# First stage of a fused attention kernel: weights fetched in column parts, x on two DMA queues, rows normalised on VectorE, and one bias transpose moved to a later stage

## The chip, the cores and the metric

The kernel runs on one core of a Trainium2 chip. A core has five engines that each take their own instructions in order: TensorE (PE, with weight loads shown apart as PEld), VectorE (DVE), ScalarE (ACT), GpSimd (POOL) and SyncE (SP), and 16 DMA engines that move data between device memory and the on-chip memory. A DMA is issued by an engine's instruction stream; here nearly all are issued by SP. The metric is the device time of one execution in microseconds (us); the times shown are medians of several executions.

## The reference

The reference is a stack of four small transformer blocks in float32, applied to x of shape (8, 112, 256) with a context of shape (8, 375, 192):

```
L0:  x += Attn(LN(x), LN(x));  x += Attn(LN(x), ctx);  x += (a * gelu(gate)) @ Wf      16 heads of 64
L1:  the same with other weights and tanh-gelu                                        16 heads of 64
L2:  x += Attn(LN(x), ctx)                                                            16 heads of 64
L3:  x += SelfAttn(LN(x)), masked, biased;  x += Attn(LN(x), ctx), masked, biased;
     x += gelu(LN(x) @ W1 + b1) @ W2                                                  16 heads of 16
```

Attn(h, c) is softmax(q k^T * scale) v with q = h Wq, k = c Wk, v = c Wv over 16 heads, then a product with Wo and a bias. Only block L3 has biases on its q and k projections. That makes ten stages, numbered 0 to 9: self, cross, ff, self, cross, ff, cross, self, cross, ff. Stage 0 is the self-attention of L0 and stage 6 is the attention of L2.

## The kernel before

**Tiles.** The 896 rows of x lie in seven tiles of 128 rows (`x_sb[t]`, loaded at L319 by seven DMAs of 128 KB). For each stage `norm(st, t)` (L495) computes mean and variance of a tile on VectorE (`st`, `mv`, `ve`, lines 498 to 502), the inverse root `rs` on GpSimd (L504), the normalised rows `xn` on GpSimd (L506), and then adds the output bias row of the stage into the tile (L507, GpSimd). The function behind `add_norm_transposes` transposes `xn` on TensorE (L520) and evicts it with the norm's gain and bias into `hT` (L299 on ScalarE or L307 on VectorE). Tiles go in groups 0 and 1, 2 and 3, 4 and 5, 6. Projections to q and k (L581) work on column blocks of two batches (j = 0 to 3); values (L605) on one batch and half of the heads; scores (`S`, L818), softmax (L783 maximum, L793 exponential, L803 reciprocal, L804 normalisation on GpSimd), transposes of the probabilities (`T`, L837) and the product with the values (`PV`, L857) work on eight heads of one batch in stages 0 and 3. The work of 16 such steps fills stage 0.

**Order.** TensorE's instructions stand in the order in which the program emits them (`manual_schedule`). The order is made while the program is built, by the class `Plan`: every piece of work is an `Item` with a cost, a deadline (in steps), the tiles that it uses and makes, and dependences with delays. The main loop emits S, T and PV of the steps and fills between them with the ready item of the earliest deadline. `plan.now` is the planner's own clock and `plan.ev` the time on it at which a piece was done; nothing of this exists on the chip. The instructions of the other engines are put in order by the framework's scheduler; on each engine they then run in that order, and one that waits holds those behind it. That scheduler goes by its own estimates: a load without dependences can stand far ahead of the place where the program emits it. The two `rv` rows, which come after the masks of the last block in the list of loads, are issued at 42.56 and 43.03 us, long before the masks.

**Loads.** Weights live in a ring of seven buffers. Loads are `Item`s in a first-in-first-out list; `pump` issues the first one as soon as its ring has room. All of them are issued by SP: Wq1, Wk1 and Wv1 of block L0 (L370, each [256, 1024] as one DMA of 1 MB with rows of 4 KB), the context in three parts (`cn`, L412, 125 partitions with pieces of 768 bytes), Wo1 (L370, rows of 1 KB) between the first two of them, then bias rows (L402) and two value-bias rows (`rv`, L1121 and L1123). The framework uses eight completion semaphores for these DMAs in turn, so that a DMA is issued when the one eight before it has landed.

**Biases of the last block.** `brows` holds the q and k biases of L3, 16 rows of 64 values. It is cleared on GpSimd (L343), loaded by a DMA that GpSimd issues (L344), scaled on GpSimd (L345, L346), transposed on TensorE (L349) and copied to `bcols` (L350). In the program this stands ahead of everything else on TensorE but the transpose of the norm vectors (`vrows`, L331). `bcols` is first used in stage 7.

Of the kernel before, what the change touches and what calls it, by code (L numbers as in the profile page):

```python
# [12 lines left out]
ALU = mybir.AluOpType  # L13
AX = mybir.AxisListType

B, T, D = 8, 112, 256
S, DC = 375, 192
# [3 lines left out]
P = 128  # L21
# [241 lines left out]
def kernel(ctx: ExitStack, tc: tile.TileContext, a: dict, out: bass.AP):  # L263
    nc = tc.nc
# [17 lines left out]
    def mm_tile():  # L282
        return ps_m.tile([P, 512], F32, tag="mm", name="mm")

    plan = Plan(RINGS)
    load = {"act": 0.0, "dve": 0.0}

    def busy(eng, us):
# [25 lines left out]
    xflat = a["x"].rearrange("b t d -> (b t) d")  # L314
    oflat = out.rearrange("b t d -> (b t) d")
    x_sb = []
    for t in range(NT):
        xt = const.tile([P, D], F32, name=f"x{t}")
        nc.sync.dma_start(xt, xflat[t * P : (t + 1) * P, :])  # L319
        x_sb.append(xt)  # L320

    ident = const.tile([P, P], F32, name="ident")
# [17 lines left out]


    brows = const.tile([16, 4, 32], F32, name="brows")
    nc.gpsimd.memset(brows, 0.0)  # L343
    nc.gpsimd.dma_start(brows[:, :, 0:16], a["padb"].rearrange("r (h d) -> r h d", d=16))  # L344
    nc.gpsimd.tensor_scalar_mul(brows[0:8, :, :], brows[0:8, :, :], 0.25)  # L345
    nc.gpsimd.memset(brows[0:8, :, 16:17], 1.0)  # L346
    bcols = const.tile([P, 16], F32, name="bcols")
    pt1 = mm_tile()
    nc.tensor.transpose(pt1[:, :16], brows.rearrange("r h d -> r (h d)"), ident[:16, :16])  # L349
    nc.vector.tensor_copy(bcols, pt1[:, :16])  # L350

    hT = const.tile([P, 2, B * T], F32, name="hT")

# [9 lines left out]
    got = {}  # L363


    def add_w(key, name, cols=None, kp=P):
        def fn():
            w = a[name] if cols is None else a[name][:, cols]
            t = wpool.tile([kp, w.shape[0] // kp, w.shape[1]], F32, tag="w", name=name)
            nc.sync.dma_start(t, w.rearrange("(c p) n -> p c n", p=kp))  # L370
            got[key] = t

        plan.add_load(Item(("load", key), 0, fn, makes=[key]))
# [24 lines left out]
    def add_row(key, name):  # L398
        def fn():
            t = rpool.tile([P, D], F32, tag="row", name="row")  # L400
            r = ROWS.index(name)
            nc.sync.dma_start(t, a["rows"][r : r + 1, :].to_broadcast([P, D]))  # L402
            got[key] = t

        plan.add_load(Item(("load", key), 0, fn, makes=[key]))
# [56 lines left out]
    def add_masks():  # L462
# [16 lines left out]
        def put_mask():  # L479
# [7 lines left out]
                 deps=[(("kj", 6, B - 1, u), 0) for u in range(4)] + [(("vj", 6, B - 1, i), 0) for i in range(3)],  # L487
                 seg=SEG[7])
        )
# [5 lines left out]
    def norm(st, t):  # L495
        xt = x_sb[t]
        s6 = small.tile([P, 6], F32, tag="st", name="st")
        nc.vector.bn_stats(s6, xt)
        mv = small.tile([P, 2], F32, tag="mv", name="mv")
        nc.vector.bn_aggr(mv, s6)  # L500
        ve = small.tile([P, 1], F32, tag="ve", name="ve")
        nc.vector.tensor_scalar_add(ve, mv[:, 1:2], EPS)  # L502
        rs = small.tile([P, 1], F32, tag="rs", name="rs")
        nc.gpsimd.tensor_tensor(rs, ve, mhalf, ALU.pow)  # L504
        xn = xpool.tile([P, D], F32, tag="xn", name="xn")
        nc.gpsimd.tensor_scalar(xn, xt, mv[:, 0:1], rs, ALU.subtract, ALU.mult)  # L506
        nc.gpsimd.tensor_add(xt, xt, got[("row", st)])  # L507
        busy("dve", 0.8)
        xns[(st, t)] = xn

    def add_norm_transposes(st, g, bt, deadline, first=False):
        for gi, ts in enumerate(GROUPS):

            def fn(gi=gi, ts=ts):
# [8 lines left out]
                for c in range(2):  # L523
# [7 lines left out]
                    ("hT", st, gi), 0.22 * len(ts), fn, deadline(gi),  # L531
                    deps=[(("norm", st, t), 4.5) for t in ts], seg=SEG[st],
                )
# [205 lines left out]
    def add_context_transposes(deadline):  # L739
        for b in range(B):  # L740
            key = ("w", "ctx", b // 3)

            def fn(b=b, key=key):
                cn = got[key]
                cols = slice(b * S, (b + 1) * S)
                for k0, kl, dst in ((0, KA, ctxA), (KA, KB, ctxB)):
                    pc = mm_tile()
                    for c in range(3):
                        nc.tensor.transpose(
                            pc[:kl, c * CH : (c + 1) * CH],  # L750
                            cn[:, (b % 3) * 3 + c, k0 : k0 + kl], ident[:CH, :CH],
                        )
                    evac(dst[:kl, cols], pc[:kl, :S], S)
                nc.sync.dma_start(ctxB[KB:, cols], ctxB[:KB, cols])

            plan.add(Item(("ctxT", b), 0.7, fn, deadline(b), uses=[key]))

# [204 lines left out]


    info = []
    SEG = [0, 0, 0, 1, 1, 1, 2, 2, 2, 2]
    for kind, dh in (
        ("self", 64), ("cross", 64), ("ff", 0), ("self", 64), ("cross", 64), ("ff", 0),
        ("cross", 64), ("self", 16), ("cross", 16), ("ff", 0),  # L970
# [1 line left out]
        st = len(info)  # L972
# [19 lines left out]
    def self_stage(st, names, wq, wk, wv, wo):  # L992
        kind, first, per, dh = info[st]
        L3 = dh == 16
        us = 2 if L3 else 4
# [65 lines left out]
    def w(name):  # L1061
        return ("w", name)
# [9 lines left out]
    st = 0  # L1072
    for bi, (L, n) in enumerate(seq):
        s0, s1, s2 = st, st + 1, st + 2
        add_row(("row", s0), n[4])
        for i in range(3):
            add_w(w(n[i]), n[i])
        if bi == 0:
            add_ctx(0, [0, 1, 2])
        add_w(w(n[3]), n[3])  # L1080
        if bi == 0:
            add_ctx(1, [3, 4, 5])
            add_ctx(2, [6, 7])
        add_w(w(n[7]), n[7])
        add_ctx_w(w(n[8]), n[8], True)
        add_ctx_w(w(n[9]), n[9], False)
        add_row(("row", s1), n[11])
        add_w(w(n[10]), n[10])
        add_w(("w", n[14], "g"), n[14], slice(FF, 2 * FF))
        add_w(("w", n[14], "a"), n[14], slice(0, FF))  # L1090
        add_row(("row", s2), n[16])
        add_w(w(n[15]), n[15])

        f0, f1, f2 = info[s0][1], info[s1][1], info[s2][1]
        add_norm_transposes(s0, n[5], n[6], hT_by(s0))
        self_stage(s0, n, w(n[0]), w(n[1]), w(n[2]), w(n[3]))
        add_products(s0, s1, w(n[3]), 8, after_pv(f0, 2), norm_by(s1))
        add_norm_transposes(s1, n[12], n[13], hT_by(s1))
        if bi == 0:
            add_context_transposes(lambda b: f1 + 4 * b - 5 if b > 1 else 7 + b)  # L1100
        cross_stage(s1, w(n[7]), w(n[8]), w(n[9]), 0.125, None)
        add_products(s1, s2, w(n[10]), 8, after_pv(f1, 4), norm_by(s2))
        add_norm_transposes(s2, n[17], n[18], hT_by(s2))
        ff_stage(s2, ("w", n[14], "a"), ("w", n[14], "g"), n[19],
                 AF.Gelu if bi == 0 else AF.Gelu_apprx_tanh, f2 - 1)
        add_products(s2, s2 + 1, w(n[15]), 8, after_ff(s2), ff_norm_by(f2))
        st += 3
# [6 lines left out]
    add_ctx_w(w(L + "Wv"), L + "Wv", False)  # L1114
    add_w(w(L + "Wo"), L + "Wo")
    add_masks()
    L3 = "L3_xattn_"

    def add_rvs():
# [38 lines left out]
    for t in range(NT):  # L1158
        norm(0, t)
        plan.refs[("row", 0)] = plan.refs.get(("row", 0), 0)  # L1160
        plan.ev[("norm", 0, t)] = 1.0

    cuts = [0, info[2][1], info[5][1], len(steps)]
    for seg in range(3):
# [11 lines left out]
        for i in range(lo - 2, hi):  # L1176
# [6 lines left out]
            if lo <= i + 1 < hi:  # L1183
                n = steps[i + 1]
# [44 lines left out]
```

## Time and profile before

| What | us |
|---|---|
| median of three runs | 1757.38 (1756.21 to 1757.70) |
| profiled execution | 1756.8 |
| its span | 1755.0 |
| TensorE busy in the span | 1696.6 (97%) |
| start of the first projection matmul (L581) | 23.55 |
| start of the first GpSimd normalisation (L804) | 46.75 |
| start of the first probability transpose (L837) | 52.75 |

A line of the profile gives the source line, the engine, the operation, what it writes and reads, the count, the busy time and the mean duration of one; behind the bar stands the idle time of the engine just before it and what ended that. In a timeline the columns are start, duration, engine and line, and in brackets the idle time before with what released it. "SPq" is the instruction stream of SP, where a DMA's duration is the time that its issue held SP. The span leaves out 1.8 us that the profiled execution's own time holds.

### The profile page before, as it was taken

Reading aid. Unit: us, or ns where it says so; the run is one execution under the profiler, and the core shown is the slowest. Engines: PE = TensorE matmul, PEld = TensorE weight load, DVE = VectorE, ACT = ScalarE, POOL = GpSimd, SP = SyncE. Lnnn points to the kernel's source line nnn. Section 1 sums busy time; section 2 is a strip of 40 time slices with the busy share of each in tenths; the row PEclk is TensorE's granted clock in tenths of the full one; section 3 lists DMA queues with packets and bytes.
Section 4 is the critical chain, followed back from the end, with each engine's and each line's share of the span. In section 5 each row is a group of like instructions: output and inputs, shape, how many; then the busy total and the mean of one; then the engine's idle time right before and its main releaser. Section 6 shows DMA issues by size and latency. Waiting matters only on the chain.

```text
span 1755.0 us, 30348 instructions
## 1 busy us (share of the span) xinstructions
PE 1696.6 (97%) x11886; PEld 1186.7 (68%) x11886; DVE 874.6 (50%) x2046; ACT 756.1 (43%) x2410; POOL 906.6 (52%) x825
## 2 busy tenths in 40 slices
PE   5999999999999999999999999999999998999989
PEld 4877766666658887666666656666666876666656
DVE  1454454555522444554555522445555588666740
ACT  2553443444521544434444431444444366555641
POOL 4223455566702322655466612645566845888880
PEclk9999999999999999999999999999999999999999
DMA  5011011000101101000000101100000101000000
GB/s 176 11 48 53 3 29 54 25 1 1 49 27 43 28 10 40 25 28 1 25 1 1 43 28 9 10 1 1 7 1 7 12 9 55 1 1 2 1 1 22
DMA packets 39464, 39.12 MB, mean 22 GB/s; under 512 B 16928, under 2 KB 34568, under 8 KB 39321
## 3 DMA queue, kind: packets, MB, share of 16 engines
q1 hardware_dynamic: 39257, 37.13, 7.6%
q8 instruction: 94, 1.54, 0.4%
q14 instruction: 49, 0.40, 0.1%
q0 software_dynamic: 64, 0.05, 0.0%
HBM read 35.48 MB, written 0.92 MB: 21 GB/s over the span
## 4 chain that ended last, share of the span: by engine, by line
PE 85%; POOL 6%; ACT 4%; DVE 4%; issue 1%; DMA 0%; SPq 0%; ACTq 0%; POOLq 0%; DVEq 0%
PE mm L581 11%; PE mm L549 11%; PE mm L837 9%; PE s L818 9%; PE mm L857 9%; PE mm L677 7%; PE mm L643 7%; PE mm L1030 7%; PE mm L686 4%; PE mm L652 4%; POOL pr L800 4%; PE mm L605 3%; ACT pr L793 3%; DVE nm L783 2%; POOL xn L506 1%; PE mm L728 1%
## 5 line engine op out<-in xcount | busy, mean ns | idle before, releaser
L800 POOL TENSOR_SCALAR pr<-pr,rinv 112x375 f32<-112x375 f32 x512 | 623.5, 1236 | 366.2 <-DVE rinv L799 362.8
L793 ACT ACTIVATE pr<-s,nm 112x375 f32<-112x375 f32 (+1 forms) x768 | 373.5, 501 | 240.4 <-DVE nm L783 166.6
L783 DVE TENSOR_REDUCE nm<-s 112x2 f32<-112x750 f32 (+1 forms) x288 | 266.2, 953 | 68.3 <-PE s L818 63.9
L837 PE MATMUL mm<-ident,pr 112*128 112x112 f32 (+2 forms) x1920 | 241.3, 265 | 13.1 <-POOL pr L800 5.2
L837 PEld LDWEIGHTS mm<-ident,pr 112*128 112x128 f32 (+2 forms) x1920 | 214.5, 152 | 58.3 <-issue 15.5
L303 ACT COPY wT<-mm 128x448 f32<-128x448 f32 (+2 forms) x285 | 150.1, 534 | 190.5 <-PE mm L837 190.2
L857 PEld LDWEIGHTS mm<-wT,v 128*64 128x64 f32 (+5 forms) x3840 | 160.3, 129 | 84.6 <-issue 32.5
L804 POOL TENSOR_TENSOR pr<-pr,rinv 112x896 f32<-112x896 f32 x48 | 80.8, 1683 | 253.7 <-DVE rinv L803 228.1
L818 PE MATMUL s<-kT,qT 64*112 64x375 f32 (+3 forms) x1792 | 207.6, 392 | 0.0
L857 PE MATMUL mm<-wT,v 128*64 128x112 f32 (+5 forms) x3840 | 200.1, 264 | 7.4 <-ACT wT L303 4.5
L818 PEld LDWEIGHTS s<-kT,qT 64*112 64x112 f32 (+1 forms) x1792 | 113.1, 172 | 68.2 <-issue 15.3
L793 ACT ACTIVATION_READ_ACCUMULATOR pr<-s,nm 112x1 f32 x768 | 158.0, 206 | 0.0
L799 DVE RECIPROCAL rinv<-sums 112x1 f32<-112x1 f32 x512 | 83.4, 163 | 98.7 <-ACT pr L793 88.1
L311 DVE COPY kT<-mm 128x375 f32<-128x375 f32 (+1 forms) x117 | 65.5, 560 | 133.4 <-PE mm L652 114.4
L311 DVE COPY wT<-mm 128x448 f32<-128x448 f32 (+2 forms) x195 | 118.6, 612 | 21.3 <-PE mm L837 18.2
L311 DVE COPY v<-mm 128x512 f32<-128x512 f32 (+2 forms) x75 | 51.8, 691 | 141.2 <-PE mm L686 118.7
L303 ACT COPY kT<-mm 128x375 f32<-128x375 f32 (+1 forms) x107 | 51.1, 478 | 129.0 <-PE mm L652 115.3
L504 POOL TENSOR_TENSOR rs<-ve,mhalf 128x1 f32<-128x1 f32 x70 | 39.4, 564 | 126.1 <-DVE ve L502 123.9
L553 DVE TENSOR_TENSOR x<-mm,x 128x256 f32<-128x256 f32 x70 | 29.5, 422 | 143.2 <-PE mm L549 143.1
L643 PE MATMUL mm<-ctxA,L_xattn_Wk 128*128 128x375 f32 x256 | 91.5, 480 | 0.0
L677 PE MATMUL mm<-L_xattn_Wv,ctxA 128*128 128x512 f32 (+1 forms) x192 | 90.7, 595 | 0.4 <-ACT hT L299 0.4
L506 POOL TENSOR_SCALAR xn<-x,mv,rs 128x256 f32<-128x256 f32 x70 | 85.8, 1226 | 7.7 <-PE mm L520 1.1
(130 smaller groups left out, 2349.4 us busy)
## 6 DMA issues: line engine op xcount, KB each, us to landing
L_xattn_Wq<-in_L_xattn_Wq_dram SPq DMA_DIRECT2D x3, 1024.0 KB, 6.7
L_xattn_Wo<-in_L_xattn_Wo_dram SPq DMA_DIRECT2D x3, 1024.0 KB, 15.9
L_xattn_w_ff<-in_L_xattn_w_ff_dram SPq DMA_DIRECT2D x3, 1024.0 KB, 5.6
L_xattn_Wp<-in_L_xattn_Wp_dram SPq DMA_DIRECT2D x2, 1024.0 KB, 7.5
L_xattn_wq<-in_L_xattn_wq_dram SPq DMA_DIRECT2D x2, 1024.0 KB, 5.0
L_xattn_wo<-in_L_xattn_wo_dram SPq DMA_DIRECT2D x2, 1024.0 KB, 5.7
L_xattn_mlp_w<-in_L_xattn_mlp_w_dram SPq DMA_DIRECT2D x2, 1024.0 KB, 4.9
cn<-in_ctx_dram SPq DMA_DIRECT2D x2, 843.8 KB
```

The costliest lines, as they stand in the source:

```text
L303: nc.scalar.copy(dst, src)
L311: nc.vector.tensor_copy(dst, src)
L549: nc.tensor.matmul(ps[:, :D], lhsT=oT[:, c, t * P : (t + 1) * P], rhs=got[w][:, c, :], start=(c == 0), stop=(c == n - 1),)
L581: nc.tensor.matmul(ps[:, i * 2 * T : (i + 1) * 2 * T], lhsT=got[w][:, k, m * P : (m + 1) * P], rhs=hT[:, k, lo:hi], start=(k == 0), stop=( ...
L643: nc.tensor.matmul(ps[:, :S], lhsT=got[w][:, (2 * u + i) * P : (2 * u + i + 1) * P], rhs=ctxA[:, cols], start=True, stop=False,)
L677: nc.tensor.matmul(ps[: KCH[c][1], :], lhsT=lhs(ctxA, slice(0, KA), c), rhs=got[w][:, hf * 512 : (hf + 1) * 512], start=True, stop=False,)
L783: nc.vector.tensor_reduce(nm[:, :, :ns], sv, AX.X, ALU.max, negate=True)
L793: nc.scalar.activation(pr[:, bk, sl, :], sv[:, bk, sl, :], AF.Exp, bias=nm[:, bk, sl : sl + 1], accum_out=sums[:, bk, sl : sl + 1],)
L800: nc.gpsimd.tensor_scalar_mul(pr[:, bk, sl, :], pr[:, bk, sl, :], rinv[:, bk, sl : sl + 1])
L818: nc.tensor.matmul(tiles[i][:, n % 2, (n // 2) * nk : (n // 2 + 1) * nk], lhsT=qap(h), rhs=kap(h), start=True, stop=True,)
L837: nc.tensor.transpose(pt[:kl, i * T : (i + 1) * T], cell[h][:, c * P : c * P + kl], ident[:T, :T])
L857: nc.tensor.matmul(po[p0 : p0 + dp, blk * T : (blk + 1) * T], lhsT=got[vk][:kl, hv * dp : (hv + 1) * dp], rhs=wt, start=(c == 0), stop=(c ...
```

## The change

Five things are done, all in the first stage but the last one:

1. The first two tiles of x are loaded through SP, the other five and the bias row of stage 0 through ScalarE's DMA queue.
2. Wq1 and Wk1 of block L0 are loaded as four DMAs of 256 columns each, Wv1 as two of 512 columns.
3. In stage 0 `xn` is computed on VectorE instead of GpSimd.
4. The planner is told that the norms of stage 0 end one after another (1.0 + 2.0 t on its clock) and that its clock stands at 9.0 when the steps begin; the context transposes of batch b may not be emitted before step 1 + b // 3.
5. The load and the scaling of `brows` become a load item in the list of loads, behind the masks and ahead of the value-bias rows, with the DMA issued by SP. The transpose into `bcols` becomes an item of stage 6.

```diff
-        nc.sync.dma_start(xt, xflat[t * P : (t + 1) * P, :])
+        (nc.sync if t < 2 else nc.scalar).dma_start(xt, xflat[t * P : (t + 1) * P, :])
...
     brows = const.tile([16, 4, 32], F32, name="brows")
-    nc.gpsimd.memset(brows, 0.0)
-    nc.gpsimd.dma_start(brows[:, :, 0:16], a["padb"].rearrange("r (h d) -> r h d", d=16))
-    nc.gpsimd.tensor_scalar_mul(brows[0:8, :, :], brows[0:8, :, :], 0.25)
-    nc.gpsimd.memset(brows[0:8, :, 16:17], 1.0)
     bcols = const.tile([P, 16], F32, name="bcols")
-    pt1 = mm_tile()
-    nc.tensor.transpose(pt1[:, :16], brows.rearrange("r h d -> r (h d)"), ident[:16, :16])
-    nc.vector.tensor_copy(bcols, pt1[:, :16])
+
+    def load_brows():
+        nc.gpsimd.memset(brows, 0.0)
+        nc.sync.dma_start(brows[:, :, 0:16], a["padb"].rearrange("r (h d) -> r h d", d=16))
+        nc.gpsimd.tensor_scalar_mul(brows[0:8, :, :], brows[0:8, :, :], 0.25)
+        nc.gpsimd.memset(brows[0:8, :, 16:17], 1.0)
+
+    def put_bcols():
+        pt1 = mm_tile()
+        nc.tensor.transpose(pt1[:, :16], brows.rearrange("r h d -> r (h d)"), ident[:16, :16])
+        nc.vector.tensor_copy(bcols, pt1[:, :16])
...
-    def add_w(key, name, cols=None, kp=P):
+    def add_w(key, name, cols=None, kp=P, parts=1):
         def fn():
             w = a[name] if cols is None else a[name][:, cols]
+            n = w.shape[1] // parts
             t = wpool.tile([kp, w.shape[0] // kp, w.shape[1]], F32, tag="w", name=name)
-            nc.sync.dma_start(t, w.rearrange("(c p) n -> p c n", p=kp))
+            for i in range(parts):
+                c = slice(i * n, (i + 1) * n)
+                nc.sync.dma_start(t[:, :, c], w[:, c].rearrange("(c p) n -> p c n", p=kp))
             got[key] = t
...
-            nc.sync.dma_start(t, a["rows"][r : r + 1, :].to_broadcast([P, D]))
+            (nc.scalar if key[1] == 0 else nc.sync).dma_start(t, a["rows"][r : r + 1, :].to_broadcast([P, D]))
...
-        nc.gpsimd.tensor_scalar(xn, xt, mv[:, 0:1], rs, ALU.subtract, ALU.mult)
+        (nc.vector if st == 0 else nc.gpsimd).tensor_scalar(xn, xt, mv[:, 0:1], rs, ALU.subtract, ALU.mult)
...
-            plan.add(Item(("ctxT", b), 0.7, fn, deadline(b), uses=[key]))
+            plan.add(Item(("ctxT", b), 0.7, fn, deadline(b), uses=[key], deps=[(("S", 1 + b // 3), 0)]))
...
-            add_w(w(n[i]), n[i])
+            add_w(w(n[i]), n[i], parts=1 if bi else (4, 4, 2)[i])
...
     add_masks()
+    plan.add_load(Item(("load", "brows"), 0, load_brows))
+    plan.add(Item(("bcols", 0), 0.1, put_bcols, info[6][1] + 8, deps=[(("load", "brows"), 10.0)], seg=SEG[6]))
...
-        plan.ev[("norm", 0, t)] = 1.0
+        plan.ev[("norm", 0, t)] = 1.0 + 2.0 * t
+    plan.now = 9.0
```

## The prediction

> **What bounds the kernel now.** I read the page's busy times first: TensorE works 97% of the span, so time is won only where TensorE stands still, and that is at the start. The stretches of the first 60 us show it (us, then busy time of PE, PEld, DVE, ACT, POOL with counts, granted clock, DMA share, GB/s):
>
> ```profile
> PE 1696.6 (97%) x11886; PEld 1186.7 (68%) x11886; DVE 874.6 (50%) x2046; ACT 756.1 (43%) x2410; POOL 906.6 (52%) x825
> 0.00:16.00 16.00, 0.36 (x1) 0.18 (x1) 4.62 (x22) 1.28 (x1) 12.23 (x25) 1.00 0.75 263
> 16.00:23.55 7.55, 4.09 (x14) 2.45 (x15) 1.41 (x4) 1.69 (x3) 6.52 (x7) 1.00 0.36 103
> 23.55:27.87 4.32, 4.32 (x13) 3.92 (x13) 0.81 (x2) 1.00 (x2) 1.05 (x2) 1.00 0.89 245
> 27.87:52.75 24.88, 24.88 (x142) 22.03 (x141) 4.88 (x7) 10.14 (x37) 1.68 (x1) 1.00 0.30 84
> ```
>
> Until 23.55 TensorE does 4.45 us of transposes; from there it never pauses. The chain that ended last, in its first 24 us, says why: the bias row's DMA (4.01 to 10.28), then GpSimd's row additions, `rs`, `brows` and `xn` up to 23.24, each `xn` 1.21 us. The weights are not what is late: Wq1, issued at 4.49, lands 8.5 us later, at 13.0. So up to 12 us can be won here, 0.7%.
>
> The second thing to read is SP, because the change moves a DMA onto it, and the groups of the bias row and GpSimd:
>
> ```profile
> 5.99 1.01 SPq L412 DMA_DIRECT2D cn<-in_ctx_dram  x1
> 7.04 15.86 SPq L370 DMA_DIRECT2D L_xattn_Wo<-in_L_xattn_Wo_dram  x1
> 22.95 13.54 SPq L412 DMA_DIRECT2D cn<-in_ctx_dram  x2
> 36.54 5.98 SPq L402 DMA_DIRECT2D row<-in_rows_dram  x2
> ...
> L402 SPq DMA_DIRECT2D row<-in_rows_dram x1: 5507/5507/5507, 36.5 to 36.5; - x1
> DMA to landing us min/median/max: 11.1/11.1/11.1
> ...
> 46.75 1.68 POOL L804 TENSOR_TENSOR pr<-pr,rinv 112x896 f32<-112x896 f32 x1 [22.14 <-DVE rinv L803]
> 52.75 0.55 PE L837 MATMUL mm<-ident,pr 112*112 112x112 f32 x4
> ```
>
> SP is held for 35 us: each DMA behind a context part is taken only when that part is nearly through, and the bias row issued at 36.54 lands at 36.54 + 11.1 = 47.6. Between 28 and 37 us, with a context part alone in flight, the DMA share is 0.34 at 100 GB/s. The last two lines give the slack of the first softmax: normalised at 48.43, read by TensorE (T of step 0) at 52.75, so 4.3 us to spare.
>
> **What the Trainium skill says.** "DMA: Bandwidth & Descriptors", section "Why a DMA increments its semaphore by 16 and not by 1": a DMA uses the largest number of engines up to 16 that divides the slowest dimension of both sides. 125 context partitions give 5 engines, and 5/16 = 0.31 agrees with the 0.34; the 16 rows of `brows` give all 16, the five busy ones among them. The same page, "Issuing engines are not separate DMA queues": the second queue saves issue time, not bandwidth; no run here shows it yet. "TensorE: Matmul & The Clock Gate", Part 1: after some 3.4 us of idleness the array runs at half clock until a window of that length has been busy. The trace agrees: the first 11 projection matmuls last 581 ns (23.55 to 27.87), those after 352.
>
> **The change part by part.**
>
> *Start of TensorE.* Only the transposes of tiles 0 and 1 now stand before the first projections. On VectorE, `xn` of 128x256 comes after all seven statistics (7 x 0.43 + `mv`, `ve`: some 4.3 us from 2.9, so 7.2). No row prices `xn` there: below by 0.2 us, half the 0.42 of the two-tensor addition of that shape (L553); above by the 1.21 of GpSimd. I take 0.4. But in VectorE's order the first eviction of its half of `hT` stands behind `xn` of tiles 3 and 4, and that of tile 4 waits for an `rs` that GpSimd makes after four row additions of 0.71: 7.6 + 0.7 x 4 + 0.55 + 0.4 + 0.55 = 12 us, or 14.5 if the row lands as late as 10.3 again. Projections then start at 12 to 14.5 instead of 23.55.
>
> *Weights in parts.* Rows of 1 KB go at 253 GB/s at a DMA share of 0.92 (24 to 28 us, Wo1), so 275 at full share; rows of 4 KB at 384 (8 to 14 us). x, row, Wq1, Wk1 are 3.15 MB: 10.9 us at 290; Wv1, 1.05 MB in rows of 2 KB, at 340 (between the two): 3.1. From 2.0 this ends at 16.0, about when the weights end now (share 0.41 in 16 to 18). The parts are on time: TensorE needs the last of Wk1 at 24, Wv1 at 26. What follows is shifted by 0 to +2 us; I take +0.5.
>
> *`brows`: the part that decides.* GpSimd's order in the built program is: four `rs`, `brows` clear, additions to tiles 0 to 3, three `rs`, addition to tile 4, **scaling of `brows`**, clear, additions to tiles 5 and 6, then the softmax normalisations. The scaling waits for the DMA of `brows`, and that stands on SP behind all three context parts, Wo1 and the next bias row. So it lands just after that row: 47.6 + 0.1 + 0.5 = 48.2. Everything behind it on GpSimd waits: 0.75 (scaling 0.55, clear 0.10, gaps), two additions 1.40, normalisation of step 0 1.69, together 3.9 and 0.1 to TensorE: T of step 0 starts at L + 4.0 = 52.2 with L the landing. Before it was 52.75. TensorE comes to it at about 12 + 2.1 (half clock) + its work of 27 = 41 to 44 and stands still for 8 to 11 us: the whole gain of the start is spent there.
>
> *What is left at that point.* Up to T of step 0 the old order does 14 projection groups, 2 value tiles and all 14 transposes; the new one 12, 3 and 8. Still to do: 2 x 1.51 - 1.72 + 6 x 0.19 = +2.4 us. And TensorE has gone cold: from 23.55 to 27.87 half clock cost 4.3/2 = 2.15; I take the same again, between 1.7 and 3.4 by the page's windows, 0 if idleness doesn't cool it.
>
> *The rest at nothing.* The removed transpose of `brows` at the head (0.28) lay in TensorE's idle time; in stage 6 it is 0.3 us of TensorE at most. The planner's new order ends with stage 0; all later work stands in the same order but for `bcols` and its neighbours in stage 6. Six DMA issues on ScalarE, 0.43 each, end by 5, before its first work at 7.1. Context transposes come at 75 us and later, their data by 48. Behind the wait on GpSimd, the exponentials of step 1 go on, its normalisation follows that of step 0 by 1.69, and its T comes some 8 us later, so there is no second stall.
>
> *Sum.* (52.2 - 52.75) + 2.4 + 2.15 = +4.0 us on the profiled execution: span 1759.0, its time 1760.8. It lies 0.6 under the median of the runs, so the median becomes 1757.4 + 4.0 = 1761.4.
>
> **The rivals.** *A shorter stall.* If `brows` lands two us after SP takes it (42.1 + 2.4 = 44.5), as it would if its pieces met no queue, T starts at 48.5: -4.25 + 2.4 + 2.15 = +0.3, and with no cooling -1.9: 1755.5 to 1757.7. Against it: all four rows issued between 36 and 43 us land 5.8 to 11.1 us after issue.
>
> *GpSimd isn't held.* The change does what it seems to do: T of step 0 starts when TensorE reaches it, 41.5 to 44: -11.2 + 2.4 = -8.9, or -6.4: 1748.5 to 1751. This needs L below 37.5 to 40, so that GpSimd is through by then; the balance with cooling is L - 44.2, so faster by 0.2% needs L below 40.7. For it: the start really frees 9 to 12 us. Against it: SP isn't free before 42, unless the context parts go through faster than now.
>
> *A longer stall.* Weight parts at 240 GB/s instead of 290 put 2.5 us on L: 1764.
>
> **How the numbers follow.** Long stall as worked out: 0.6, own range 1758.5 to 1764.5 (shift -0.5 to +2, cooling 0.7 to 3.4). Shorter stall: 0.23. GpSimd not held: 0.13. Longer stall: 0.04. A measurement of this kernel can tell about 0.2%, 3.5 us, from no change. Slower by more, above 1760.9: two thirds of the first case and all of the last, 0.45. Faster: the third case, 0.13. Between: 0.42. The range 1754 to 1766 leaves out the third case and little else.
>
> **What would show it.** Right: GpSimd's line for the scaling of `brows` with a wait of 25 us or more on the DMA; projections from 12 to 14.5; one pause of TensorE of 8 to 11 us ahead of the first L837 transposes near 52, matmuls of 581 ns after it. Wrong: first normalisation on GpSimd before 42, no pause, or `cn` parts through by 35. Also wrong: 1 KB parts that arrive so slowly that the projections wait for Wk1.

## The result and the profile after

The changed kernel takes 1756.24 us, the median of 14 runs (1753.20 to 1759.81), beside 1756.20 (1754.35 to 1757.70) of the kernel before: a ratio of 1.0003 with a 95% interval of 0.9995 to 1.0011. No difference can be measured. The forecast of 1761.4 was 5.2 us too high: 1.2 of it because the three runs that it started from had a median of 1757.38, and 4.0 because it expected a loss where none was measured. The time lies inside its range of 1754 to 1766.

The profiled execution took 1759.81 us with a span of 1757.9, the longest of its 14 runs. Its page has this line of busy times:

```profile
PE 1703.8 (97%) x11886; PEld 1191.4 (68%) x11886; DVE 876.2 (50%) x2053; ACT 755.9 (43%) x2410; POOL 897.7 (51%) x817
```

TensorE's share is what it was, and it is busy 7 us longer with the same number of matmuls: the clock records have 31.5 us of half clock in this span and 17.1 in that of before, and half of the difference is 7.2. The records begin only at 19.7 us here and at 27.9 in the kernel before, so a granted clock of 1.00 ahead of that shows nothing. The stretches of the start, cut at the new events (us, then busy time of PE, PEld, DVE, ACT, POOL with counts, granted clock, DMA share, GB/s):

```profile
0.00:11.74 11.74, 1.49 (x6) 0.87 (x6) 5.74 (x26) 1.85 (x2) 5.52 (x16) 1.00 0.80 251
11.74:14.33 2.59, 1.11 (x2) 0.50 (x2) 0.87 (x2) 0.00 (x0) 2.59 (x5) 1.00 1.06 376
14.33:43.20 28.87, 28.79 (x142) 23.77 (x142) 5.76 (x10) 10.82 (x40) 0.77 (x2) 1.00 0.53 140
43.20:47.78 4.58, 0.03 (x2) 0.00 (x1) 0.62 (x1) 0.77 (x6) 3.69 (x5) 0.92 0.07 22
47.78:54.00 6.22, 6.22 (x21) 5.67 (x22) 0.73 (x2) 1.07 (x2) 1.68 (x1) 0.51 0.03 11
```

The projections start at 11.74 instead of 23.55, and TensorE is full from 14.33. But in the fourth row it does nothing for 4.5 us, and in the last the granted clock is 0.51. The timeline of TensorE has the same four events (start, duration, what ended the idle time before):

```profile
11.74 1.12 PE L589 MATMUL mm<-hT,L_xattn_Wq 128*128 128x224 f32 x2 [1.30 <-ACT hT L300]
14.33 2.24 PE L589 MATMUL mm<-hT,L_xattn_Wq 128*128 128x224 f32 x5 [1.48 <-DVE hT L308]
...
47.78 0.99 PE L845 MATMUL mm<-ident,pr 112*112 112x112 f32 x4 [4.55 <-POOL pr L812]
48.57 3.22 PE L589 MATMUL mm<-hT,L_xattn_Wq 128*128 128x224 f32 x8
```

(L589 was L581, L845 was L837, L812 was L804.) The first four transposes of the probabilities, T of step 0, wait for GpSimd's normalisation; the eight projection matmuls behind them last 3.22 us. GpSimd's timeline at that place names what held it:

```profile
43.97 0.56 POOL L349 TENSOR_SCALAR brows<-brows 8x128 f32<-8x128 f32 x1 [28.87 <-DMA brows<-in_padb_dram]
44.59 0.10 POOL L350 MEMSET brows<- 8x4 f32 x1
44.68 1.40 POOL L515 TENSOR_TENSOR x<-x,row 128x256 f32<-128x256 f32 x2
46.04 1.68 POOL L812 TENSOR_TENSOR pr<-pr,rinv 112x896 f32<-112x896 f32 x1
```

GpSimd stands 28.87 us in front of the scaling of `brows`, 4 KB that nobody needs before stage 7, with two row additions and the normalisation behind it. The reciprocal for that normalisation was ready at 37.6. The instruction stream of SP, where the load stands:

```profile
10.34 0.40 SPq L420 DMA_DIRECT2D cn<-in_ctx_dram  x1
10.79 8.61 SPq L378 DMA_DIRECT2D L_xattn_Wo<-in_L_xattn_Wo_dram  x1
19.45 13.21 SPq L420 DMA_DIRECT2D cn<-in_ctx_dram  x2
32.70 5.09 SPq L410 DMA_DIRECT2D row<-in_rows_dram  x1
37.91 0.70 SPq L348 DMA_DIRECT2D brows<-in_padb_dram  x1
```

The order is the one of before, and SP is still held by the context parts, but the row is taken at 37.8 (end of its issue) instead of 42.0, and `brows`, 5.9 us after its issue, is in at 43.8.

**Where the gain went.** T of step 0 starts at 47.78 instead of 52.75, which is 5.0 earlier. The 128th of the 1920 matmuls of L845 is a good place to compare at, since ahead of it both orders have the same 1164 matmuls, but for the one that transposes `brows`: it starts at 189.2 before and at 189.7 after. So all of the start's gain is given back by 190 us. At 860 us the two are still 0.4 apart; the rest of the span's difference of 2.9 arises after 1440 us, where this execution has three more stretches of half clock, in work that the change doesn't touch, and the medians don't have it.

### The profile page after: what moved, and what is told of

Its sections match the earlier page's. It is cut to its first block, busy times and chain, and to the rows that moved or that the text cites. A ratio compares the mean times of both kernels' runs of the same rounds, so it can differ in the third digit from the quotient of the medians.

```text
span 1757.9 us, 30363 instructions
## 1 busy us (share of the span) xinstructions
PE 1703.8 (97%) x11886; PEld 1191.4 (68%) x11886; DVE 876.2 (50%) x2053; ACT 755.9 (43%) x2410; POOL 897.7 (51%) x817
## 4 chain that ended last, share of the span: by engine, by line
PE 84%; POOL 5%; ACT 4%; DVE 4%; SPq 2%; issue 1%; DMA 1%; ACTq 0%; POOLq 0%; DVEq 0%
PE mm L557 11%; PE mm L589 10%; PE mm L845 10%; PE s L826 9%; PE mm L865 9%; PE mm L685 7%; PE mm L651 7%; PE mm L1037 7%; PE mm L694 4%; PE mm L660 4%; PE mm L613 3%; ACT pr L801 3%; POOL pr L808 3%; DVE nm L791 2%; PE mm L736 1%; PE mm L715 1%
## 5 line engine op out<-in xcount | busy, mean ns | idle before, releaser
L845 PE MATMUL mm<-ident,pr 112*128 112x112 f32 (+2 forms) x1920 | 242.9, 266 | 17.4 <-POOL pr L812 4.6
L845 PEld LDWEIGHTS mm<-ident,pr 112*128 112x128 f32 (+2 forms) x1920 | 215.7, 152 | 63.9 <-issue 17.2
L812 POOL TENSOR_TENSOR pr<-pr,rinv 112x896 f32<-112x896 f32 x48 | 80.8, 1683 | 232.2 <-DVE rinv L811 212.5
L312 DVE COPY v<-mm 128x512 f32<-128x512 f32 (+2 forms) x73 | 50.4, 691 | 139.1 <-PE mm L694 118.7
L589 PE MATMUL mm<-hT,L_xattn_Wq 128*128 128x224 f32 x384 | 87.2, 373 | 2.9 <-DVE hT L308 1.5
```

Source lines behind the costliest of these rows:

```text
L312: nc.vector.tensor_copy(dst, src)
L589: nc.tensor.matmul(ps[:, i * 2 * T : (i + 1) * 2 * T], lhsT=got[w][:, k, m * P : (m + 1) * P], rhs=hT[:, k, lo:hi], start=(k == 0), stop=( ...
L845: nc.tensor.transpose(pt[:kl, i * T : (i + 1) * T], cell[h][:, c * P : c * P + kl], ident[:T, :T])
```

## The experiments

The theory after the result: all of the start's gain is lost because GpSimd waits for `brows`; the pause and the half clock after it are this wait, and without it the change is worth 8 to 9 us. The rivals: the gain is lost in the order of the work (the planner's new clock), in the transfers (column parts, two queues), or the move of `brows` costs nothing and the cold array everything. All ratios are to the kernel before, measured beside each group of kernels (its medians there lie between 1755.6 and 1756.2).

| Kernel | `brows` scaled | projections from (second wait ends) | T of step 0 | 128th L845 | median us | ratio, 95% interval |
|---|---|---|---|---|---|---|
| before | 15.3 | 23.55 | 52.75 | 189.2 | 1756.20 | 1 |
| changed | 43.97 | 11.74 (14.33) | 47.78 | 189.7 | 1756.24 | 1.0003 [0.9995, 1.0011] |
| `brows` on ScalarE's queue | 15.59 | 12.19 (14.24) | 42.02 | 180.9 | 1747.65 | 0.9958 [0.9946, 0.9971] |
| `brows` as before | 14.0 | 16.76 | 45.27 | 184.2 | 1752.94 | 0.9983 [0.9975, 0.9991] |
| only `brows` moved | 47.69 | 23.26 | 52.57 | 189.0 | 1755.84 | 0.9997 [0.9989, 1.0005] |
| pause filled | 45.82 | 12.32 (14.37) | 49.63 | 190.3 | 1754.09 | 0.9994 [0.9985, 1.0002] |
| weights whole | 20.1 | 16.57 (20.03) | 49.06 | 188.0 | 1754.14 | 0.9989 [0.9982, 0.9996] |
| x on one queue | 13.8 | 10.26 (13.75) | 41.72 | 180.6 | 1749.68 | 0.9964 [0.9951, 0.9977] |
| `xn` on GpSimd | 20.6 | 13.32 (15.41) | 42.98 | 181.9 | 1748.90 | 0.9961 [0.9947, 0.9976] |
| old planner clock | 15.0 | 14.90 | 43.59 | 180.1 | 1747.97 | 0.9955 [0.9941, 0.9970] |
| one queue, weights whole | 14.1 | 12.69 | 42.10 | 181.0 | 1750.11 | 0.9964 [0.9952, 0.9977] |
| old clock, row behind weights | 15.2 | 14.19 | 43.08 | 179.6 | 1746.60 | 0.9951 [0.9939, 0.9964] |
| the same, x on one queue | 13.4 | 11.42 | 40.09 | 176.6 | 1743.96 | 0.9937 [0.9925, 0.9950] |
| changed, whole, one queue | 45.46 | 12.63 (14.30) | 49.28 | 191.0 | 1757.60 | 1.0014 [1.0007, 1.0020] |

### `brows` on another queue

```diff
-        nc.sync.dma_start(brows[:, :, 0:16], a["padb"].rearrange("r (h d) -> r h d", d=16))
+        nc.scalar.dma_start(brows[:, :, 0:16], a["padb"].rearrange("r (h d) -> r h d", d=16))
```

> The changed kernel with one word altered: the DMA of brows is issued on ScalarE's queue, behind the bias row of stage 0, and so lands before the context parts. Theory (GpSimd held behind brows, then a cold array): the first normalisation on GpSimd follows its reciprocal at 37 to 38 us, T of step 0 starts when TensorE reaches it, at 43 to 44 instead of 47.8, and no half clock follows: -4.4 - 3.0 = -7.4 us against the changed kernel, 1749, ratio to the kernel before 0.995 to 0.997. Rival (the start's gain is lost to the new order of work or to the weight parts, and GpSimd's wait lies beside something else): ratio 0.999 to 1.001 as for the changed kernel.

Measured: 1747.65 us, ratio 0.9958 [0.9946, 0.9971]. The timeline of GpSimd in this kernel:

```profile
15.59 0.56 POOL L349 TENSOR_SCALAR brows<-brows 8x128 f32<-8x128 f32 x1 [1.28 <-DMA brows<-in_padb_dram]
...
36.62 1.68 POOL L812 TENSOR_TENSOR pr<-pr,rinv 112x896 f32<-112x896 f32 x1 [1.24 <-DVE rinv L811]
```

and that of TensorE:

```profile
40.51 1.68 PE L589 MATMUL mm<-hT,L_xattn_Wk 128*128 128x224 f32 x8
42.02 0.55 PE L845 MATMUL mm<-ident,pr 112*112 112x112 f32 x4
42.41 1.69 PE L589 MATMUL mm<-hT,L_xattn_Wq 128*128 128x224 f32 x8
```

One word in one line: the wait of 28.87 us is 1.28, the normalisation starts at 36.62 instead of 46.04, the four transposes follow the projections with no idle time, and eight projection matmuls last 1.69 us instead of 3.22. The rest of the program is that of the changed kernel. So the wait for `brows` is what the start's gain was spent on. This kernel also gives the remaining work apart from the cold clock: from T of step 0 to the 128th L845 matmul it takes 138.9 us, the kernel before 136.5 and the changed kernel 141.9. The order costs 2.4 and the cold array 3.0.

### `brows` where it was, and `brows` alone

The second kernel is the changed one with `brows` loaded by GpSimd and transposed ahead of everything, as before:

```diff
-        nc.sync.dma_start(brows[:, :, 0:16], a["padb"].rearrange("r (h d) -> r h d", d=16))
+        nc.gpsimd.dma_start(brows[:, :, 0:16], a["padb"].rearrange("r (h d) -> r h d", d=16))
...
+    load_brows()
+    put_bcols()
...
-    plan.add_load(Item(("load", "brows"), 0, load_brows))
-    plan.add(Item(("bcols", 0), 0.1, put_bcols, info[6][1] + 8, deps=[(("load", "brows"), 10.0)], seg=SEG[6]))
```

> The changed kernel with the brows part undone: its DMA issued by GpSimd and its transpose at the head of TensorE's order, as before; everything else as changed. Theory: GpSimd isn't held after 15 us, T of step 0 isn't late, but TensorE's first transposes wait for brows at the head (it lands at 13.3 in the kernel before), so projections start at 16 to 19 instead of 12 to 14: 1750 to 1754, ratio 0.996 to 0.999, between the run with brows on ScalarE's queue and the kernel before. Rival: 0.999 to 1.001.

Measured: 0.9983 [0.9975, 0.9991]. TensorE's timeline shows why it isn't the whole gain:

```profile
14.78 0.28 PE L354 MATMUL mm<-ident,brows 16*128 16x16 f32 x1 [7.73 <-POOL brows L350]
14.99 1.11 PE L531 MATMUL mm<-ident,xn 128*128 128x128 f32 x4
16.76 3.44 PE L592 MATMUL mm<-hT,L_xattn_Wq 128*128 128x224 f32 x8 [0.66 <-ACT hT L300]
```

The transposes of `xn` stand behind that of `brows`, so projections start 4.6 us later than with `brows` on ScalarE's queue (16.76 beside 12.19), and T of step 0 comes 3.25 later. To take the transpose away from the head is right; where the load went is what spoilt it.

The third is the kernel before with the move of `brows` as its only edit.

> The kernel before with only the brows part of the change (DMA on SP in the list of loads, transpose in stage 6). Theory: brows lands at 47.6 to 48.3, GpSimd's first normalisation ends at 50.5 to 52.4, and TensorE comes to T of step 0 at 52 to 52.75, so the late load costs 0 to 0.5 us there, and the head of TensorE wins up to 0.7 us: ratio 0.999 to 1.0005. Rival (the brows part costs time by itself, wherever TensorE starts): ratio above 1.002.

Measured: 0.9997 [0.9989, 1.0005]. GpSimd's timeline:

```profile
47.69 0.54 POOL L348 TENSOR_SCALAR brows<-brows 8x128 f32<-8x128 f32 x1 [24.15 <-DMA brows<-in_padb_dram]
48.29 0.10 POOL L349 MEMSET brows<- 8x4 f32 x1
48.35 1.67 POOL L808 TENSOR_TENSOR pr<-pr,rinv 112x896 f32<-112x896 f32 x1
```

The same wait, 24 us long, costs nothing here: the normalisation moves from 46.75 to 48.35, and TensorE reads it at 52.57. It lies in the 4.3 us of slack that the late start left. The move is harmful only together with the parts that make the start early.

### The pause filled

Five matmuls of 128x512 on the first weight, whose product goes nowhere, stand ahead of T of step 0 in the changed kernel; they keep the array busy. In the timeline they are ten instructions of L845, and T is L849.

```diff
         def emit_t(bank):
+            if s == 0 and bank[0][0] == 0:
+                pw = mm_tile()
+                for _ in range(5):
+                    nc.tensor.matmul(pw, lhsT=got[("w", "L0_xattn_Wq1")][:, 0, :P], rhs=got[("w", "L0_xattn_Wq1")][:, 0, :512], start=True, stop=True)
             pt = mm_tile()
```

> The changed kernel with five extra matmuls of 128x512, their product not used, just ahead of T of step 0, some 4.3 us of TensorE work in the place of its pause of 4.5 us. Theory (the pause costs its length and then half clock for 6 us): T of step 0 starts at 47.8 as in the changed kernel or up to 0.5 later, the matmuls after it take 352 ns instead of 581, and the time falls by 2.5 to 3: ratio to the kernel before 0.998 to 0.999. Rival (the half clock has another cause, or costs nothing because another engine sets the pace there): the ratio stays at 1.000 to 1.001.

Measured: 0.9994 [0.9985, 1.0002]. TensorE's timeline:

```profile
43.05 4.46 PE L845 MATMUL mm<-L_xattn_Wq 128*128 128x512 f32 x10
49.63 0.59 PE L849 MATMUL mm<-ident,pr 112*112 112x112 f32 x4 [2.13 <-POOL pr L812]
50.06 2.92 PE L589 MATMUL mm<-hT,L_xattn_Wq 128*128 128x224 f32 x8
```

In this execution `brows` came at 45.7, 1.9 us later than in the profile of the changed kernel, though the loads are the same, so 2.13 us of pause were left after the filler, and T of step 0 came at 49.63 and not by 48.3 as expected. The clock records show half clock from 50.4 to 53.8, 3.4 us; in the changed kernel from 47.0 to 53.8, 6.8 us. From T of step 0 to the 128th L845 matmul it takes 140.6 us: the cold array cost 1.7 instead of 3.0. Both are half of the time in which TensorE worked at half clock (3.4 and 6.1 us). So cooling is a part of the loss and the later T of step 0 the larger one: of the 8.8 us between the changed kernel and the one with `brows` on ScalarE's queue at the 128th L845 matmul, 3.0 are cooling and 5.8 the later T. The forecast took some 3.4 us of idleness as what cools the array; here a single pause of 2.13 us was followed by half clock, although TensorE had worked without a break before it and again from 49.63. The filler was only partly a test: it showed the price of a half-clock window, not of none, and the ratio lies between the ranges of the two expectations.

### One part of the start at a time

The kernels of this part start from the one with `brows` on ScalarE's queue (0.9958). The weights as whole DMAs again:

```diff
-            add_w(w(n[i]), n[i], parts=1 if bi else (4, 4, 2)[i])
+            add_w(w(n[i]), n[i], parts=1)
```

> As the run with brows on ScalarE's queue (ratio 0.9958, T of step 0 at 42.0), but the three weights as one DMA of 1 MB each, rows of 4 KB. Theory (the parts decide nothing once GpSimd is free): Wq1 lands at 9 to 10.5 and Wk1 at 12.5 to 13.5, TensorE needs them at 12.2 and 16.7, T of step 0 stays at 42 to 43, ratio 0.9955 to 0.997. For the context chain: if the parts are what brought it forward by 4 us in the changed kernel, the bias row behind the context parts lands near 47.6 as before; if not, near 44. Rival (early weight parts are what lets TensorE start at 12 to 14): T at 45 or later, ratio above 0.997.

Measured: 0.9989 [0.9982, 0.9996]; the expectation of my theory failed, and three quarters of the gain are gone. VectorE's timeline shows the statistics of the last tiles of x:

```profile
9.94 0.43 DVE L506 BATCH_NORM_STATS2 st<-x 128x6 f32<-128x256 f32 x1 [2.72 <-DMA x<-in_x_dram]
...
11.59 0.43 DVE L506 BATCH_NORM_STATS2 st<-x 128x6 f32<-128x256 f32 x1 [1.11 <-DMA x<-in_x_dram]
13.36 0.43 DVE L506 BATCH_NORM_STATS2 st<-x 128x6 f32<-128x256 f32 x1 [1.34 <-DMA x<-in_x_dram]
```

With parts, the last of the seven starts at 8.98. Here the last tile of x, 128 KB, is in at 13.3 (fifteen of its sixteen pieces by 12.1), and TensorE waits for the norms:

```profile
16.57 1.11 PE L589 MATMUL mm<-hT,L_xattn_Wq 128*128 128x224 f32 x2 [1.29 <-ACT hT L300]
20.03 2.23 PE L589 MATMUL mm<-hT,L_xattn_Wq 128*128 128x224 f32 x5 [2.35 <-DVE hT L308]
```

x, in rows of 1 KB on ScalarE's queue, competes with the weights on SP's, and these differ in two ways from before: their rows have 4 KB instead of 1 KB, and by 4 us SP has issued 2 MB of them instead of 0.5. Which of the two delays x isn't shown. The next kernel leaves the parts and puts x and the first row on SP, ahead of the weights:

```diff
-        (nc.sync if t < 2 else nc.scalar).dma_start(xt, xflat[t * P : (t + 1) * P, :])
+        nc.sync.dma_start(xt, xflat[t * P : (t + 1) * P, :])
...
-            (nc.scalar if key[1] == 0 else nc.sync).dma_start(t, a["rows"][r : r + 1, :].to_broadcast([P, D]))
+            nc.sync.dma_start(t, a["rows"][r : r + 1, :].to_broadcast([P, D]))
```

> As the run with brows on ScalarE's queue, but x and the bias row of stage 0 all on SP, ahead of the weight parts, as before. Theory: the two queues save issue time of 2.5 us for the weights and nothing for x: the first projections start within 1 us of 12 to 14, T of step 0 at 42 to 43, ratio 0.9955 to 0.997. Rival (two queues are needed for the early start): T at 44 or later, ratio above 0.997. For the context chain: if the second queue is what brought it forward, the bias row behind it lands near 47.6.

Measured: 0.9964 [0.9951, 0.9977], the same as with two queues within the intervals. Both edits together:

> The load of brows on ScalarE's queue; x and the first bias row all on SP, ahead of the weights; the three weights whole, in rows of 4 KB. Theory (whole weights hurt only because they crowd out x on the other queue): x lands first, Wq1 near 13, Wk1 near 15.6; T of step 0 at 42 to 44 us; ratio to the kernel before 0.996 to 0.9975. Rival (the parts are needed for themselves, since the first columns of Wq1 come late): T of step 0 at 46 or later, ratio 0.9985 or more.

Measured: 0.9964 [0.9952, 0.9977], T of step 0 at 42.10. The numbers of the expectation hold. With x first on one queue, whole weights cost nothing; with x on a second queue, they cost 0.3% (0.9989 beside 0.9958), 7.0 us at T of step 0. The column parts are the remedy for a harm that whole weights do only together with the second queue. The Trainium skill, "DMA: Bandwidth & Descriptors", section "Issuing engines are not separate DMA queues", says that DMAs of all issuing engines interleave on the same 16 DMA engines; the trace agrees: whole weights on SP's queue made the last tile of x on ScalarE's 4.4 us late.

The two other edits of the start, undone one by one:

```diff
-        (nc.vector if st == 0 else nc.gpsimd).tensor_scalar(xn, xt, mv[:, 0:1], rs, ALU.subtract, ALU.mult)
+        nc.gpsimd.tensor_scalar(xn, xt, mv[:, 0:1], rs, ALU.subtract, ALU.mult)
```

> As the run with brows on ScalarE's queue, but xn of stage 0 on GpSimd as before. Theory (only tiles 0 and 1 stand before the first projections; xn takes 1.21 us there instead of 0.36 to 0.41, but VectorE's eviction of hT no longer stands behind xn of tile 4): the transposes start 1 to 2 us later and the projections go on without the second wait; T of step 0 at 42 to 44, ratio 0.9955 to 0.998. Rival (xn on VectorE is the main gain): T at 46 or later, ratio above 0.998.

Measured: 0.9961 [0.9947, 0.9976], projections from 13.32 and T of step 0 0.95 us later. In the runs no difference to `xn` on VectorE (0.9958) can be seen.

```diff
-        plan.ev[("norm", 0, t)] = 1.0 + 2.0 * t
-    plan.now = 9.0
+        plan.ev[("norm", 0, t)] = 1.0
...
-            plan.add(Item(("ctxT", b), 0.7, fn, deadline(b), uses=[key], deps=[(("S", 1 + b // 3), 0)]))
+            plan.add(Item(("ctxT", b), 0.7, fn, deadline(b), uses=[key]))
```

> As the run with brows on ScalarE's queue, but the planner's clock, norm times and context dependence as before, so that all 14 transposes of stage 0 stand ahead of the first projection. Theory: the first projection waits for xn of tile 6 behind GpSimd's additions and starts at 15.5 to 18; T of step 0 comes 3.5 to 6 us later than 42.0 but with 2.6 us less work left, so the time is 1 to 3 us above: ratio 0.9965 to 0.9975. Rival (the planner's new order is the main gain): ratio above 0.998.

Measured: 0.9955 [0.9941, 0.9970], better than the 0.9965 to 0.9975 of the expectation, which had T of step 0 3.5 to 6 us later. It comes at 43.59 instead of 42.02, but the 128th L845 matmul at 180.1 instead of 180.9: the order of before has more of its work done by T of step 0 and loses nothing. The planner's new clock is worth nothing that can be measured.

### A better start

Where the projections stop a second time, as in the kernel with `brows` on ScalarE's queue, they wait for VectorE's `xn` of tile 4, and this for its `rs` (1.40 us), which GpSimd makes behind four row additions (L515). Here the first bias row is loaded by SP behind the three weights, so that GpSimd makes all seven `rs` first; old planner clock, `brows` on ScalarE's queue.

```diff
-        add_row(("row", s0), n[4])
+        if bi:
+            add_row(("row", s0), n[4])
         for i in range(3):
             add_w(w(n[i]), n[i], parts=1 if bi else (4, 4, 2)[i])
         if bi == 0:
+            add_row(("row", s0), n[4])
             add_ctx(0, [0, 1, 2])
```

> The load of brows on ScalarE's queue, the planner's clock and norm times as in the kernel before, and the first bias row loaded by SP behind the three weights instead of ahead of them. Theory (what holds the first projections now is the rs of tile 4, behind four row additions on GpSimd): without a row to add, GpSimd makes all seven rs first; first projections at 12 to 13 us without a pause after them, ratio 0.9935 to 0.995. Rival (x itself is late): no earlier than 14, ratio 0.9955 as with the row ahead.

Measured: 0.9951 [0.9939, 0.9964]; projections from 14.19 and not from 12 to 13, which is a miss: the interval doesn't part it from the run with the row ahead (0.9955). x on two queues is late as well: the statistics of its last tile start at 9.19, and with x on one queue by 6.5. With x on SP:

> As the run with the row behind the weights, and all of x on SP, ahead of the weights. Theory: x lands before any weight, so the first projections start at 10.5 to 12 us; ratio 0.993 to 0.995, about 1744 to 1747 us. Rival (the weights are late when x comes first): 0.9955 or more.

Measured: 1743.96 us, 0.9937 [0.9925, 0.9950], a ratio as expected. TensorE's timeline:

```profile
7.22 1.97 PE L528 MATMUL mm<-ident,xn 128*128 128x128 f32 x8 [2.82 <-DVE xn L514]
9.91 1.72 PE L528 MATMUL mm<-ident,xn 128*128 128x128 f32 x6 [0.72 <-DVE xn L514]
11.42 3.33 PE L589 MATMUL mm<-hT,L_xattn_Wq 128*128 128x224 f32 x8
14.54 1.78 PE L589 MATMUL mm<-hT,L_xattn_Wk 128*128 128x224 f32 x8
```

All 14 transposes stand ahead of the projections, which start at 11.42, and nothing stands still from there to T of step 0. T of step 0 starts at 40.09, 12.7 us before that of the kernel before, with the same work left (136.5 to the 128th L845 matmul): this is the 12 us that the profile of before offered, and it beats both kernels.

### The forecast's own chain

The last kernel is the changed one with `brows` on SP as it is, but with whole weights and x and the row on SP, as the kernel before loads them. It asks whether the forecast's sum holds where the start of the loads isn't faster.

> The changed kernel with brows on SP as it is, but with the weights whole (rows of 4 KB) and x and the bias row on SP. Theory (the forecast failed by one term, the landing of brows; where the start of the loads is as slow as in the kernel before, its sum holds): brows lands at 47 to 48.2 us, T of step 0 at 51.2 to 52.2, TensorE pauses 7 to 10 us and is at half clock after it; +3 to +5 us, ratio 1.0017 to 1.003. Rival (the sum itself is wrong, or the landing does not depend on the start): ratio 1.000, brows lands near 44.

Measured: 1757.60 us, 1.0014 [1.0007, 1.0020]: slower by 2.0 us in the medians, between the two. TensorE's timeline:

```profile
40.39 1.68 PE L589 MATMUL mm<-hT,L_xattn_Wk 128*128 128x224 f32 x8
49.28 1.00 PE L845 MATMUL mm<-ident,pr 112*112 112x112 f32 x4 [7.21 <-POOL pr L812]
50.06 3.22 PE L589 MATMUL mm<-hT,L_xattn_Wq 128*128 128x224 f32 x8
```

and GpSimd's:

```profile
45.46 0.56 POOL L349 TENSOR_SCALAR brows<-brows 8x128 f32<-8x128 f32 x1 [30.40 <-DMA brows<-in_padb_dram]
```

`brows` landed at 45.3, not at 47 to 48.2, and the pause and the loss were accordingly smaller than expected (7.2 us and 2.0 instead of 7 to 10 and 3 to 5). Given that landing, the sum is right: (49.28 - 52.75) + 2.4 + 2.8 (half clock from 44.7 to 54.9, 5.7 us of it worked) = +1.7, and the 128th L845 matmul stands at 191.0 beside 189.2, +1.8. But `brows`, with the same loads in the same order as in the kernel in which it alone was moved (47.6 there), landed 2.3 us earlier here. So the way in which the loads are cut isn't by itself what sets the landing.

What does can be read from the completion events in the trace. The Trainium skill, "DMA: Bandwidth & Descriptors", section "Why a DMA increments its semaphore by 16 and not by 1", says that the engines of one DMA finish independently and that it has landed when the last has. The trace agrees: each context part has one event at its issue and then five. These are the five events of the first context part, and the sixteen of the row behind the context (the first and the last five of them), in us:

```
kernel                     first context part             row: the first ... the last five
before                     23.9 24.1 25.0 26.2 30.3       43.5 ... 44.6 44.6 44.7 44.9 47.6
only brows moved           24.6 25.1 26.6 28.1 29.6       42.8 ... 44.0 44.2 44.2 46.6 47.0
changed                    25.8 26.0 26.0 26.1 26.2       39.2 ... 43.1 43.1 43.3 43.3 43.5
changed, whole, one queue  25.6 26.3 26.6 27.4 27.5       40.4 ... 44.0 44.1 44.5 44.7 45.1
pause filled               24.8 25.2 25.5 26.0 27.4       41.5 ... 42.7 42.8 42.9 43.6 45.4
```

In the kernel before, the five engines of a context part finish over 6.4 us, in the changed kernel over 0.4; the means are alike, 25.9 and 26.0. In the kernel before one event of the row comes 2.7 us behind the other fifteen. A transfer behind the context lands when the DMA engine that is furthest behind has got to it.

The lag does more than hold back one piece. In all 14 kernels the row lands 17.0 to 18.0 us after the last event of the first context part, although that event lies anywhere from 26.0 to 30.3 us. Between the two stands SP: its issue of the row ends 0.3 to 0.9 us after the last event of the second context part (at 42.0 after 41.5 in the kernel before, at 37.8 after 37.5 in the changed one). So, by these times, the engine that is behind also sets when SP comes to the row and to `brows`. How far behind it is differs between kernels with the same loads (only `brows` moved and the last kernel: 5.0 and 1.9 us; the changed kernel and the one with the pause filled: 0.4 and 2.6). What puts an engine behind stays open; the larger spreads here are in kernels with whole weights, but not in all of them.

## Why the prediction was wrong in its size

**The bound and the place of the loss: right.** Up to 12 us of TensorE's idle start could be won (the best kernel here got 12.7 at T of step 0). The projections were forecast at 12, or at 14.5 with a late row, by the chain to VectorE's part of `hT`. That chain ended at 14.33, with the row in at 9.9; the forecast hadn't named the two matmuls on ScalarE's part, which start at 11.74 and are followed by a wait. GpSimd's scaling of `brows` waited 28.87 us where 25 or more were named, and one pause stands ahead of T of step 0 with matmuls at half speed behind it. That this wait, with the half clock after it, is what the gain was spent on is shown by the kernel with `brows` on ScalarE's queue: 180.9 instead of 189.7 at the 128th L845 matmul.

**The step that failed: the landing of `brows`, L = 48.2.** It was made of the 47.6 at which the row of before landed, 0.1, and 0.5 for slower column parts ("What follows is shifted by 0 to +2 us; I take +0.5"). L measured 43.8: the shift was -3.9 instead of +0.5. The price of the column parts isn't the cause. They were forecast to be through at 16.0, and their last piece landed at 16.7 (18.1 in the kernel before). The rate was mis-sized, since the stretch of Wo1 that it was read from has pieces of the context in it: from 7 to 9 us the trace after shows 360 GB/s at a DMA share of 1.03, against the 275 to 290 forecast; but from 2 to 7 us it shows 258, and the mean came out right. What was wrong is that I took the 47.6 for a property of the load order. It was that of one late piece in each load, which I take for one DMA engine running behind the others in that execution. The last event of the first context part came at 30.3 there and at 26.2 in the changed kernel, 4.1 us earlier, and the row's landing moved with it by the same 4.1, from 47.6 to 43.5. I read the DMA share and the issue times and not the completion events.

**What hung on L.** The rest of the chain was right: from L to T of step 0, 4.0 us, measured 4.0 (43.8 to 47.78) and again 4.0 in the last kernel. The pause was 4.55 us instead of 8 to 11, by the same 4.4 us by which T of step 0 came earlier than 52.2.

**The other terms.** Remaining work +2.4, counted from the order, measured 2.4. Cooling +2.15 (1.7 to 3.4), measured 3.0. `xn` on VectorE 0.4 us, measured 0.36 to 0.41. With the measured T, -5.0 + 2.4 + 3.0 gives the +0.5 of the 128th L845 matmul, but for rounding; it must, since 2.4 and 3.0 are differences of the same stretch, and what checks the 3.0 is half of the 6.1 us worked at half clock. The forecast's own balance, L - 44.2, gives -0.4 for L = 43.8; the medians differ by 0.04.

**The range and the rivals.** That the time lies inside the range of 1754 to 1766 owes more to its width than to the sum: it lies outside the 1758.5 to 1764.5 of the forecast's main case, to which it gave 0.6, and inside the 1755.5 to 1757.7 of a rival. That rival, the shorter stall, with L = 44.5 and +0.3, came nearest, with a chance of 0.23. Its mechanism isn't what happened: `brows` did queue, 5.9 us from its issue to its landing, but SP came to it at 37.9 and not at 42.1. "GpSimd isn't held" named 1748.5 to 1751 and L below 40.7; with L at 15.4 the kernel with `brows` on ScalarE's queue took 1747.65. The longer stall, with slow parts, is excluded: the parts were through 0.7 us later than forecast and not 2.5. What I argued against the shorter stall (the rows behind the context land 5.8 to 11.1 us after issue) spoke of the time after the issue and missed that the issue itself could move by 4 us.

**Edits at nothing.** The removed transpose of `brows` was costed at nothing, since it lay in idle time. It stayed free only as long as the start was late: left at the head of an early start, it holds the projections up until 16.76.

## What to carry to other kernels

An early start is worth only as much as the latest thing that its first dependent steps wait for: list what every engine on that path waits for in program order, and keep a load that is needed much later, with the work behind it, off an engine that is needed soon and off a queue with slow transfers. When a landing time carries a forecast, read when each DMA engine finished and not only the mean rate, and give the landing, and each issue that waits behind it, the spread of those times. Before a load is spread over two queues, put what is needed first ahead on one: here that was as fast within the intervals, and needed no column parts.

## What the runs showed of the hardware

- Loads in rows of 1 KB reached 360 GB/s (DMA share 1.03, from 7 to 9 us of the changed kernel); I had estimated 290.
- Two queues at once: the tiles of x on one queue beside whole weights on the other were complete at 13.3 us; beside weights in column parts at 9.0, and on the same queue ahead of the weights at 6.4 to 7.6. Whether the row size or the amount in flight does it is open.
- The DMA engines of one load can finish 6.4 us apart, and what stands behind it inherits that: the row behind the context landed 17.0 to 18.0 us after the last event of the first context part in all 14 kernels, and `brows` landed at 43.8 and at 45.7 us in two kernels with the same loads.
- Half clock came in stretches of 3.4 us or multiples of it (3.4, 6.8 and 10.2 us in the clock records, after pauses of 2.1, 4.6 and 7.2 us), and cost half of the time worked in them: 1.7, 3.0 and 2.8 us.
